# The last image's tail of a four-layer convolution kernel: sums by known means, a three-stage output loop, expert weights in halves

## The chip, the cores and the metric

The kernel runs on one core of a Trainium2 chip. Its time is the time on the device in microseconds (us), the median of several runs. All arithmetic is fp32. The engines are TensorE (PE in the profile; its weight loads are PEld), VectorE (DVE), ScalarE (ACT), GpSimd (POOL) and SyncE (SP), which issues most of the transfers.

## The reference

The input is x of shape (4, 256, 64, 64): four images of 256 channels and 4096 pixels. Four layers follow each other, each of the form `x = x + layer(gn(x))`, where `gn` normalises groups of 8 channels.

```python
def _gn(v, G=32, eps=1e-5):
    g = v.reshape(B_, G, C_ // G, H_, W_)
    return ((g - mean(g)) / sqrt(var(g) + eps)).reshape(v.shape)

# layer 0: 3x3 convolution, group norm of 8 groups, relu, then attention over the 4096 pixels
xs = relu(group_norm(conv3x3(x)));  attn = softmax(theta(xs)^T phi(xs));  y = attn g(xs)
layer0 = group_norm(conv1x1(y)) * 0.1 + xs
# layer 1: rmsnorm, qkv, linear attention of 4 heads, output product, rmsnorm
q = softmax(q, over head dim);  k = softmax(k, over pixels)
layer1 = rmsnorm(w_out @ (context(k, v) applied to q * scale))
# layer 2: per-image depthwise 3x3 taps and a 1x1 product, both generated from pooled hidden values
layer2 = einsum('bchw,boc->bohw', depthwise3x3(x, dk), pk) + bias
# layer 3: a mixture of 4 experts, mixed per image from the pooled input
alpha = softmax(relu(mean(x) @ w1.T) @ w2.T)
layer3 = einsum('boc,bchw->bohw', sum_k alpha_k experts_k, x)
```

## The kernel before, in words

Channels lie on the 128 partitions in two halves (`h`, NH = 2), and an image of 4096 pixels along the free dimension. PSUM is one pool of eight banks of 128x512 (`bank`). SBUF work tiles come from pools: `k4` (128x1024, nine buffers), `k2` (128x512, five). The order of the work is written out by hand, under a manual schedule: each layer is a Python generator that emits instructions and yields a number, and the class `Chain` turns the yielded numbers into steps of credit. `run` advances one chain by a step whenever the attention of another image advances by one. So attention of image b (1024 pf and 1024 py matmuls over the four images) is interleaved with the tail of image b-1 (layers 0's end to 3) and the convolution of image b+1. What a generator yields therefore decides beside which attention step its later work stands.

In `attend` (L885 to L948) a step is two pf matmuls (L895), two exponentials (L896), two py matmuls (L934) and a VectorE addition into tot (L124).

`Chain` also has a list of held products. The products of layer 3 of image 2, sixteen pieces of 128x512, are kept there; `fill(n)` emits the matmuls of n of them (L1357), and a later `settle()` their VectorE additions (res) and output transfers. They are emitted at fixed places of the last image's tail, which has no attention beside it.

The last image's tail keeps its convolution output in `x_cols`, inside the tile xp (argument `xs_in`), and its running image in tpg. It has these stages:

- `nonlocal_out` (L952 to L987): group statistics of the attention output (`group_finish`, L330: bn_aggr, matmul pm, matmul pv, a root on POOL, L217), then for each of eight parts of 1024 columns `stt` (wy times sc plus xs, a residual sum into big, here tpg) and two bn_stats (L984), whose statistics `linear_attention` needs.
- `linear_attention` (from L990): a loop of ps_qkv products, then the output loop. In it `outputs(c)` (L1086) makes four ps_o matmuls into two banks, four ScalarE squares with an accumulated sum (L1094), and the root of the sums (zr: VectorE L1096, POOL L217). `scaled` (L1100) multiplies by the root into z; in the last tail (`alone`) ScalarE does bank 0 and VectorE bank 1. `added` (L1110) transposes z (ps_zt, L1115), adds it to the image and takes bn_stats, for each half h. The order of a turn is outputs(c), added(c-1), scaled(c), settle, and after c = 2 and 4 a fill of one held product.
- `generated` (L1138): hidden products ps_h, normalised copies into xp, pooled values, taps dk; then for parts of the image the depthwise taps on VectorE (`taps`) or by diagonal matmuls (ps_dw), the weights pk from slices wp2 that SP loads, and the 1x1 products ps_pw.
- `mixed` (L1301): pooled values, alpha, expert weights wm by VectorE from the loaded experts ex, a bias b3 through the matmul ps_b (L1348), and sixteen output pieces: two ps_ex matmuls (L1357), the VectorE addition res, and an output transfer by SP.

For images 0 to 2 the same functions run beside attention, without `xs_in`, `diag` and `alone`; the expert mix of image 2 goes to `held`.

The statement that advances the output loop of a tail is this one:

```python
        last = None
        for c in range(NC):
            zb = outputs(c)
            yield 0.6
            if last is not None:
                added(c - 1, last)
            last = scaled(*zb)
            w.settle()
            if c in (2, 4):
                w.fill(1)
            yield 0.6
```

Of the kernel before, what the change touches and what calls it, by code (L numbers as in the profile page):

```python
# [8 lines left out]
F32 = mybir.dt.float32  # L9
AF = mybir.ActivationFunctionType  # L10
# [3 lines left out]
P = 128  # L14
# [79 lines left out]
def conv_preact_fast(ctx: ExitStack, tc: tile.TileContext, guard, x, wc, wtpg, ww, wqkv, wout, w1cat, wd2,  # L94
# [235 lines left out]
    def group_finish(st, avg, eps, shift=None):  # L330


        mv = sp.tile([P, NH, 2], F32, name="mv")
        for h in range(NH):
            nc.vector.bn_aggr(mv[:, h, :], st[:, h, :, :].rearrange("p c s -> p (c s)"))
        if shift is not None:
            tt(mv[:, :, 0], mv[:, :, 0], shift, ALU.add)
        yield 1
        pm = bank("pm")
        nc.tensor.matmul(pm[:, 0:NH], avg, mv[:, :, 0], start=True, stop=True)  # L340
        gm = sp.tile([P, NH], F32, name="gm")
# [608 lines left out]


    def nonlocal_out(w, b, big, k4, xs_in):  # L952
# [19 lines left out]
        _, gm, rstd = yield from group_finish(wy_stats[b], avg32, 1e-5, bias)  # L972
        sc, sh = affine(gm, rstd, vec_s[:, V_G2W, :], vec_s[:, V_G2B, :], bias, 0.1)
        st = stats_tile()
        w.fill(2)
        for i, (c, h) in enumerate(PARTS):
            cols = bass.ts(c, CH)
            wy, xs = parts[i]
            stt(big[:, h, cols], wy, sc[:, h:h + 1], xs, ALU.mult, ALU.add)
            if i + ahead < len(PARTS):  # L980
                parts.append(load_parts(i + ahead))
            yield 0.6
            for s in range(2):
                nc.vector.bn_stats(st[:, h, 2 * c + s, :], big[:, h, bass.ts(2 * c + s, 512)])  # L984
            yield 0.6
# [4 lines left out]
    def linear_attention(w, b, big, qT, k4, st, sh, alone):  # L990
# [95 lines left out]
        def outputs(c):  # L1086
            zr = sp.tile([P, 4], F32, name="zr", bufs=3)
            banks = []
            for s in range(2):
# [5 lines left out]
                banks.append(ps)  # L1095
            nc.vector.tensor_scalar(zr, zr, 1e-24, None, ALU.max)  # L1096
            rsqrt(zr, zr)
            return zr, banks

        def scaled(zr, banks):  # L1100
            z = k4("z").rearrange("p (j o) -> p j o", j=4)
            for s in range(2):
                if alone and s == 0:
                    for j in range(2):
                        nc.scalar.activation(z[:, j, :], banks[0][:, j, :], AF.Copy, scale=zr[:, j:j + 1])
                    continue
# [3 lines left out]
        def added(c, z):  # L1110
            cols = bass.ts(c, 512)
            for h in range(NH):
# [5 lines left out]

        last = None
        for c in range(NC):  # L1120
            zb = outputs(c)
            yield 0.6
# [9 lines left out]
        w.fill(2)  # L1132
# [5 lines left out]
    def generated(w, b, big, k4, st, sh, diag):  # L1138
# [126 lines left out]
        w.settle()  # L1265
# [4 lines left out]
        for n, i in enumerate(mine):  # L1270
# [9 lines left out]
            if n == 0:  # L1280
                for j in range(R):
# [19 lines left out]
    def mixed(w, b, big, k4, st, sh, held):  # L1301
# [29 lines left out]
        wm = k2("wm")  # L1331
        for j in range(NE):
            if j == 0:
                nc.vector.tensor_scalar(wm, ex[j // 2][:, j % 2, :], al[:, 0:1], None, ALU.mult)
            else:
                stt(wm, ex[j // 2][:, j % 2, :], al[:, j:j + 1], wm, ALU.mult, ALU.add)
            yield 0.5

        mix = wm.rearrange("p (h o) -> p h o", h=NH)
# [5 lines left out]
        pb3 = bank("ps_b3")  # L1345
        for oh in range(NH):
            for h in range(NH):
                nc.tensor.matmul(pb3[:, oh:oh + 1], wm[h][:, bass.ts(oh, P)], off[:, h:h + 1],  # L1348
                                 start=(h == 0), stop=(h == NH - 1))
        b3 = sp.tile([P, NH], F32, name="b3")  # L1350
        tt(b3, sh, pb3[:, 0:NH], ALU.subtract)

        def product(c, oh):
            cols = bass.ts(c, 512)
            ps = bank("ps_ex")
            for h in range(NH):
                nc.tensor.matmul(ps, wm[h][:, bass.ts(oh, P)], big[:, h, cols], start=(h == 0), stop=(h == NH - 1))  # L1357

            def added():
                res = k2("res")  # L1360
# [3 lines left out]

        w.settle()
        for c in range(N // 512):
            for oh in range(NH):
                if held is not None:
                    held.append(lambda c=c, oh=oh: lambda added=product(c, oh): added()())
                else:  # L1370
                    w.later(1, product(c, oh)())
                    yield 0.1
# [39 lines left out]
    with tc.manual_schedule(engines={E.PE, E.Activation, E.DVE, E.Pool, E.SP}):  # L1412
# [19 lines left out]
        last = end.steps()  # L1432
        while next(attention, False):
            pass
# [592 lines left out]
```

## Time and profile before

| | |
|---|---|
| median of 3 runs | 3117.1 us |
| the runs | 3116.27, 3117.1, 3123.15 us |
| the profiled execution | 3122.35 us |
| its span, first to last instruction | 3120.6 us |
| mean granted clock of TensorE | 0.987 |
| busy: PE, DVE, ACT, POOL | 3005.0, 2129.1, 1138.5, 131.1 us |
| instructions: PE, DVE, ACT, POOL | 8606, 2700, 2100, 178 |

The busy time of an engine is the sum of its instructions' durations. Since instructions overlap a little on VectorE and ScalarE, the pace of a row of equal instructions is shorter than one duration, and both are used here. A matmul of 128x512 in fp32 shows as two records. In the timeline, a line gives the start, the duration (of all that are merged), the engine, the source line, the operation, output and inputs, and in square brackets how long the engine was idle before it and what ended that. The clock is a share of full speed.

### The profile page before, as it was taken

The page shows a single profiled execution, that of the slowest core. Times are in us where ns is not written, and L with a number is a line of the kernel's source. Part 1 is how long each engine was busy: PE and PEld are TensorE (multiplying, and loading weights), DVE is VectorE, ACT ScalarE, POOL GpSimd, SP SyncE. Part 2 cuts the span into 40 slices and gives each one's busy share as a digit, 9 for nine tenths or more (in the row PEclk, how much of TensorE's full clock was granted, in tenths as well). Part 3 has the DMA queues.
Part 4 walks back from the last instruction along what each step waited for, and adds up shares of the span by engine and source line. Part 5 has one row for each costly group of instructions (what it writes and reads, how often), then busy time and mean ns, then how long its engine had stood idle before and what let it go on. Part 6 is the DMA issues. An engine that isn't in the chain of part 4 may idle for free.

```text
span 3120.6 us, 24280 instructions
## 1 busy us (share of the span) xinstructions
PE 3005.0 (96%) x8606; PEld 1487.8 (48%) x8606; DVE 2129.1 (68%) x2700; ACT 1138.5 (36%) x2100; POOL 131.1 (4%) x178
## 2 busy tenths in 40 slices
PE   6899999999999999999999999999999999996888
PEld 3354555445554444444565444444555544443533
DVE  8747777853557986786537896878353768855485
ACT  2134333353545332223454432322355453333510
POOL 0100000000110000000001000000000100000100
PEclk9999999999999999999999999999999999998999
DMA  5233111032001023113200102310510010120011
GB/s 217 80 101 136 37 48 35 26 59 88 33 11 34 7 74 125 41 44 81 88 11 1 41 29 86 104 41 24 128 48 1 11 41 7 47 74 34 14 61 65
DMA packets 58912, 174.25 MB, mean 56 GB/s; under 512 B 6432, under 2 KB 16416, under 8 KB 54560
## 3 DMA queue, kind: packets, MB, share of 16 engines
q1 hardware_dynamic: 54752, 155.85, 14.5%
q0 software_dynamic: 4032, 16.78, 2.9%
q8 instruction: 70, 1.15, 0.1%
q14 instruction: 58, 0.48, 0.0%
HBM read 111.26 MB, written 78.12 MB: 61 GB/s over the span
## 4 chain that ended last, share of the span: by engine, by line
PE 76%; DVE 17%; issue 5%; ACT 1%; POOL 0%; DMA 0%; POOLq 0%; ACTq 0%; DVEq 0%
PE pf L895 22%; PE py L934 22%; PE ps_qkv L1024 5%; PE ps_conv L496 4%; DVE dw L127 4%; PE ps_tp L871 4%; PE ps_ex L1357 3%; DVE tot L124 3%; PE ps_pw L1219 3%; PE ps_conv L568 2%; PE ps_g L876 2%; PE ps_wy L918 1%; PE ps_o L1092 1%; DVE big L127 1%; PE ps_ctx L1046 1%
## 5 line engine op out<-in xcount | busy, mean ns | idle before, releaser
L896 ACT ACTIVATE pr<-pf 128x512 f32<-128x512 f32 x1024 | 603.7, 597 | 1194.1 <-PE pf L895 1148.6
L895 PE MATMUL pf<-tpg 128*128 128x512 f32 x2048 | 968.8, 595 | 1.5 <-ACT pr L896 1.5
L934 PE MATMUL py<-pr,tpg 128*128 128x512 f32 x2048 | 962.1, 592 | 3.0 <-ACT pr L896 2.9
L124 DVE TENSOR_TENSOR tot<-tot,pr 128x1024 f32<-128x1024 f32 x448 | 546.4, 1220 | 182.6 <-ACT pr L896 181.3
L934 PEld LDWEIGHTS py<-pr,tpg 128*128 128x128 f32 x2048 | 388.9, 190 | 494.7 <-issue 478.3
L895 PEld LDWEIGHTS pf<-tpg 128*128 128x128 f32 x2048 | 382.0, 190 | 436.1 <-issue 411.4
L127 DVE SCALAR_TENSOR_TENSOR dw<-xp,dk,dw 128x1008 f32<-128x1008 f32 x216 | 273.0, 1268 | 6.8 <-ACT dw L1211 3.7
L496 PE MATMUL ps_conv<-v,u 128*128 128x512 f32 x384 | 170.8, 592 | 0.0
L1024 PE MATMUL ps_qkv<-wqkv_s,xg 128*128 128x384 f32 x384 | 129.9, 487 | 0.0
L124 DVE TENSOR_TENSOR tpg<-ps_g,bg_s 128x512 f32<-128x512 f32 x32 | 22.1, 692 | 145.6 <-PE ps_g L876 145.6
L871 PE MATMUL ps_tp<-big,wtpg_s 128*128 128x512 f32 x256 | 118.1, 605 | 3.0 <-ACT big L668 3.0
L496 PEld LDWEIGHTS ps_conv<-v,u 128*128 128x128 f32 x384 | 72.8, 190 | 92.2 <-issue 91.2
L217 POOL TENSOR_TENSOR rstd<-rstd,half 128x2 f32<-128x2 f32 x24 | 16.8, 700 | 2375.5 <-DVE rstd L351 2181.1
L1219 PE MATMUL ps_pw<-dw,pk 128*128 128x512 f32 x224 | 104.6, 601 | 8.1 <-DVE dw L127 8.1
L909 DVE RECIPROCAL inv<-pss 128x512 f32<-128x512 f32 x32 | 107.3, 3352 | 7.1 <-PE pss L907 7.1
L1024 PEld LDWEIGHTS ps_qkv<-wqkv_s,xg 128*128 128x128 f32 x384 | 72.2, 190 | 53.6 <-issue 9.3
L1034 DVE TENSOR_REDUCE qs<-qk 128x16 f32<-128x512 f32 x24 | 16.5, 686 | 118.6 <-ACT qk L1028 118.6
L872 ACT ACTIVATE tpg<-ps_tp,btp_s 128x512 f32<-128x512 f32 x64 | 43.8, 687 | 119.6 <-PE ps_tp L871 119.6
L871 PEld LDWEIGHTS ps_tp<-big,wtpg_s 128*128 128x128 f32 x256 | 47.9, 195 | 55.0 <-issue 50.6
L1094 ACT ACTIVATE junk<-ps_o 128x256 f32<-128x256 f32 x128 | 49.2, 384 | 67.5 <-PE ps_o L1092 59.4
L1219 PEld LDWEIGHTS ps_pw<-dw,pk 128*128 128x128 f32 x224 | 43.0, 192 | 62.6 <-issue 52.0
L1028 ACT ACTIVATE qk<-ps_qkv,rinv 128x256 f32<-128x256 f32 x96 | 45.6, 475 | 72.4 <-PE ps_qkv L1024 61.6
(309 smaller groups left out, 3120.7 us busy)
## 6 DMA issues: line engine op xcount, KB each, us to landing
xp<-in_x_dram SPq DMA_DIRECT2D x16, 1024.0 KB, 6.3
wy_d<-wt SPq DMA_DIRECT2D x32, 512.0 KB, 3.0
out_dram<-res SPq DMA_DIRECT2D x64, 256.0 KB, 2.0
wy<-wy_d SPq DMA_DIRECT2D x28, 512.0 KB, 4.7
xs_d<-big POOLq DMA_DIRECT2D x24, 512.0 KB, 11.0
u<-filters SPq DMA_DIRECT2D x48, 256.0 KB, 2.5
xs<-xs_d SPq DMA_DIRECT2D x24, 512.0 KB, 5.3
u<-rows_d SPq DMA_DIRECT2D x36, 256.0 KB, 3.1
```

The source lines that it names most:

```text
L124: nc.vector.tensor_tensor(o, a, b, op)
L127: nc.vector.scalar_tensor_tensor(o, a, s, b, op0, op1)
L496: nc.tensor.matmul(ps[oh], u(oh, h), v[:, bass.ts(h, 512)], start=(h == 0), stop=(h == NH - 1))
L568: nc.tensor.matmul(ps[:, bass.ts(oh, IY * IX)], u[i][:, h, bass.ts(oh, P)], v[:, i, bass.ts(h, IY * IX)], start=(h == 0), stop=(h == NH - 1))
L871: nc.tensor.matmul(ps, wtpg_s[:, h, k, :], big[:, h, cols], start=(h == 0), stop=(h == NH - 1))
L895: nc.tensor.matmul(pf, phi[:, bass.ts(2 * m + s, P)], theta[:, bass.ts(q, 512)], start=True, stop=True)
L896: nc.scalar.activation(pr[:, bass.ts(s, 512)], pf, AF.Exp)
L909: nc.vector.reciprocal(inv, pss)
L934: nc.tensor.matmul(py, g[:, bass.ts(2 * m + s, P)], probs[i][:, bass.ts(s, 512)], start=(m == 0 and s == 0), stop=(m == NM - 1 and s == 1))
L1024: nc.tensor.matmul(ps[:, 0:3 * HID], xg[:, h, bass.ts(j, P)], wqkv_s[:, h, :], start=(h == 0), stop=(h == NH - 1))
L1219: nc.tensor.matmul(ps, pk[:, h * NH * P + oh * P:h * NH * P + (oh + 1) * P], dw[h][:, bass.ts(s, 512)], start=(h == 0), stop=(h == NH - 1))
L1357: nc.tensor.matmul(ps, wm[h][:, bass.ts(oh, P)], big[:, h, cols], start=(h == 0), stop=(h == NH - 1))
```

## The change

It has five parts.

1. In the last attention, a generator `residual_sums` has ScalarE copy each 512 columns of `x_cols` to a scratch tile with an accumulated sum, three times in each attention step; VectorE adds the sixteen sums into res_sum.
2. In `nonlocal_out` of the last image, the mean of the residual sum is formed from known means before the sum itself. After each of the eight sums ScalarE takes the squares about that mean with an accumulator. The sixteen bn_stats and the bn_aggr are gone; `group_finish` calls `moments` in their place.
3. The output loop of the last image has three stages: outputs(c+1), scaled(c), added(c-1). The root of c+1 stands between the two halves of added(c-1). ScalarE scales three quarters (j = 0, 1, 2), VectorE one.
4. In `generated` the held results are settled after the first part's taps and no longer ahead of them.
5. In `mixed`, for all images, alpha times rstd is formed first, and the weights in two halves of four operations on 256 columns. For images without `held`, the first four banks get the products of half 0, then the bias product, then half 1.

```diff
     def group_finish(st, avg, eps, shift=None):
-        mv = sp.tile([P, NH, 2], F32, name="mv")
-        for h in range(NH):
-            nc.vector.bn_aggr(mv[:, h, :], st[:, h, :, :].rearrange("p c s -> p (c s)"))
+        if callable(st):
+            mv = st()
+        else:
+            mv = sp.tile([P, NH, 2], F32, name="mv")
+            for h in range(NH):
+                nc.vector.bn_aggr(mv[:, h, :], st[:, h, :, :].rearrange("p c s -> p (c s)"))
...
+    def residual_sums(xs_in):
+        parts = sp.tile([P, NH, N // 512], F32, name="res_parts", bufs=1)
+        for h in range(NH):
+            for c in range(N // 512):
+                nc.scalar.activation(junk(), xs_in[:, h, bass.ts(c, 512)], AF.Copy, accum_out=parts[:, h, c:c + 1])
+                yield
+        nc.vector.tensor_reduce(res_sum, parts, AX.X, ALU.add)
...
+        if xs_in is not None:
+            tt(mv[:, :, 0], wmv[:, :, 0], bias, ALU.subtract)
+            tt(mv[:, :, 0], mv[:, :, 0], sc, ALU.mult)
+            stt(mv[:, :, 0], res_sum, 1.0 / N, mv[:, :, 0], ALU.mult, ALU.add)
+            nc.vector.tensor_scalar(centre, mv[:, :, 0], -1.0, None, ALU.mult)
+
+            def moments():
+                nc.vector.tensor_reduce(mv[:, :, 1], squares, AX.X, ALU.add)
+                nc.vector.tensor_scalar(mv[:, :, 1], mv[:, :, 1], 1.0 / N, None, ALU.mult)
+                return mv
+            st = moments
...
-            for s in range(2):
-                nc.vector.bn_stats(st[:, h, 2 * c + s, :], big[:, h, bass.ts(2 * c + s, 512)])
+            if xs_in is not None:
+                nc.scalar.activation(wy, big[:, h, cols], AF.Square, bias=centre[:, h:h + 1], accum_out=squares[:, h, c:c + 1])
+            else:
+                for s in range(2):
+                    nc.vector.bn_stats(st[:, h, 2 * c + s, :], big[:, h, bass.ts(2 * c + s, 512)])
...
+            if alone:
+                for j in range(4):
+                    src = banks[j // 2][:, j % 2, :]
+                    if j < 3:
+                        nc.scalar.activation(z[:, j, :], src, AF.Copy, scale=zr[:, j:j + 1])
+                    else:
+                        nc.vector.tensor_scalar(z[:, j, :], src, zr[:, j:j + 1], None, ALU.mult)
+                return z
...
+        if alone:
+            this, last = outputs(0), None
+            root(this[0])
+            for c in range(NC):
+                after = outputs(c + 1) if c + 1 < NC else None
+                z = scaled(*this)
+                for h in range(NH):
+                    if last is not None:
+                        added(c - 1, last, (h,))
+                    if h == 0 and after is not None:
+                        root(after[0])
+                this, last = after, z
+                w.settle()
+                if c in (2, 4):
+                    w.fill(1)
+                yield 1
+            added(NC - 1, last)
+            w.fill(2)
+            return st
...
         dw = {mine[0]: centre(mine[0])}
-        w.settle()
...
             if n == 0:
+                w.settle()
                 for j in range(R):
...
-        wm = k2("wm")
-        for j in range(NE):
-            if j == 0:
-                nc.vector.tensor_scalar(wm, ex[j // 2][:, j % 2, :], al[:, 0:1], None, ALU.mult)
-            else:
-                stt(wm, ex[j // 2][:, j % 2, :], al[:, j:j + 1], wm, ALU.mult, ALU.add)
-            yield 0.5
...
-            nc.vector.tensor_scalar(wm[h], mix[:, h, :], rstd[:, h:h + 1], None, ALU.mult)
-        yield 1
+        for h in range(NH):
+            nc.vector.tensor_scalar(scales[:, h, :], al, rstd[:, h:h + 1], None, ALU.mult)
...
+            for j in range(NE):
+                e = ex[j // 2].rearrange("p k (h o) -> p k h o", h=NH)[:, j % 2, h, :]
+                if j == 0:
+                    nc.vector.tensor_scalar(wm[h], e, scales[:, h, 0:1], None, ALU.mult)
+                else:
+                    stt(wm[h], e, scales[:, h, j:j + 1], wm[h], ALU.mult, ALU.add)
+                if j % 2 == 1:
+                    yield 0.6
+        yield 0.5
...
+        first = [bank("ps_ex") for _ in range(4)]
+        for h in range(NH):
+            for ps, (c, oh) in zip(first, pieces):
+                multiply(ps, c, oh, h)
+            if h == 0:
+                bias()
+        for ps, (c, oh) in zip(first, pieces):
+            w.later(1, adder(ps, c, oh)())
+            yield 0.1
...
+        sums = residual_sums(x_cols)
         while next(attention, False):
+            for _ in range(3):
+                next(sums, None)
+        for _ in sums:
             pass
```

More of the change, by code (lines that the diff above doesn't have):

```diff
@@ L948, in attend @@
                 yield
+    res_sum = cp.tile([P, NH], F32, name="res_sum")
+    def residual_sums(xs_in):
[5 more added lines that the diff above has]
+        nc.vector.tensor_reduce(res_sum, parts, AX.X, ALU.add)
     def nonlocal_out(w, b, big, k4, xs_in):
@@ L971, in nonlocal_out @@
         bias = vec_s[:, V_WB, :]
-        _, gm, rstd = yield from group_finish(wy_stats[b], avg32, 1e-5, bias)
+        wmv, gm, rstd = yield from group_finish(wy_stats[b], avg32, 1e-5, bias)
         sc, sh = affine(gm, rstd, vec_s[:, V_G2W, :], vec_s[:, V_G2B, :], bias, 0.1)
         st = stats_tile()
+        if xs_in is not None:
+            mv = sp.tile([P, NH, 2], F32, name="mv_in", bufs=1)
+            centre = sp.tile([P, NH], F32, name="centre", bufs=1)
+            squares = sp.tile([P, NH, N // CH], F32, name="squares", bufs=1)
+            tt(mv[:, :, 0], wmv[:, :, 0], bias, ALU.subtract)
[7 more added lines that the diff above has]
+            st = moments
         w.fill(2)
@@ L1095, in outputs, with root, added @@
                 banks.append(ps)
+            return zr, banks
+        def root(zr):
             nc.vector.tensor_scalar(zr, zr, 1e-24, None, ALU.max)
             rsqrt(zr, zr)
-            return zr, banks
         def scaled(zr, banks):
             z = k4("z").rearrange("p (j o) -> p j o", j=4)
+            if alone:
[6 more added lines that the diff above has]
+                return z
             for s in range(2):
[L1103 to L1106, printed above, removed]
                 tt(z[:, bass.ts(s, 2), :], banks[s], zr[:, bass.ts(s, 2)].unsqueeze(2).to_broadcast([P, 2, NH * P]), ALU.mult)
             return z
-        def added(c, z):
+        def added(c, z, halves=range(NH)):
             cols = bass.ts(c, 512)
-            for h in range(NH):
+            for h in halves:
                 pt = bank("ps_zt")
@@ L1121, in linear_attention @@
             zb = outputs(c)
+            root(zb[0])
             yield 0.6
@@ L1131, in linear_attention @@
         added(NC - 1, last)
-        w.fill(2)
         return st
@@ L1330, in mixed @@
         w.fill(3)
-        wm = k2("wm")
-        for j in range(NE):
-            if j == 0:
-                nc.vector.tensor_scalar(wm, ex[j // 2][:, j % 2, :], al[:, 0:1], None, ALU.mult)
-            else:
-                stt(wm, ex[j // 2][:, j % 2, :], al[:, j:j + 1], wm, ALU.mult, ALU.add)
-            yield 0.5
-        mix = wm.rearrange("p (h o) -> p h o", h=NH)
+        scales = sp.tile([P, NH, NE], F32, name="scales")
+        for h in range(NH):
+            nc.vector.tensor_scalar(scales[:, h, :], al, rstd[:, h:h + 1], None, ALU.mult)
+        mix = k2("wm").rearrange("p (h o) -> p h o", h=NH)
         wm = []
@@ L1342, in mixed, with bias, multiply, adder @@
             wm.append(mix[:, h, :] if held is None else filter_tile("wmh")[:, 0, :])
-            nc.vector.tensor_scalar(wm[h], mix[:, h, :], rstd[:, h:h + 1], None, ALU.mult)
-        yield 1
[L1345 to L1349, printed above, removed]
-        b3 = sp.tile([P, NH], F32, name="b3")
[L1351 to L1357, printed above, removed]
+            for j in range(NE):
[7 more added lines that the diff above has]
+        yield 0.5
+        b3 = sp.tile([P, NH], F32, name="b3")
+        def bias():
+            pb3 = bank("ps_b3")
+            for oh in range(NH):
+                for h in range(NH):
+                    nc.tensor.matmul(pb3[:, oh:oh + 1], wm[h][:, bass.ts(oh, P)], off[:, h:h + 1],
+                                     start=(h == 0), stop=(h == NH - 1))
+            tt(b3, sh, pb3[:, 0:NH], ALU.subtract)
+        def multiply(ps, c, oh, h):
+            nc.tensor.matmul(ps, wm[h][:, bass.ts(oh, P)], big[:, h, bass.ts(c, 512)], start=(h == 0), stop=(h == NH - 1))
+        def adder(ps, c, oh):
             def added():
-                res = k2("res")
+                res, cols = k2("res"), bass.ts(c, 512)
                 stt(res, ps, b3[:, oh:oh + 1], big[:, oh, cols], ALU.add, ALU.add)
@@ L1363, in product @@
             return added
-        w.settle()
[L1366 to L1372, printed above, removed]
+        def product(c, oh):
+            ps = bank("ps_ex")
+            for h in range(NH):
+                multiply(ps, c, oh, h)
+            return adder(ps, c, oh)
+        pieces = [(c, oh) for c in range(N // 512) for oh in range(NH)]
+        if held is not None:
+            bias()
+            for c, oh in pieces:
+                held.append(lambda c=c, oh=oh: lambda added=product(c, oh): added()())
+            return
+        w.settle()
+        first = [bank("ps_ex") for _ in range(4)]
+        for h in range(NH):
+            for ps, (c, oh) in zip(first, pieces):
+                multiply(ps, c, oh, h)
+            if h == 0:
+                bias()
+        for ps, (c, oh) in zip(first, pieces):
+            w.later(1, adder(ps, c, oh)())
+            yield 0.1
+        for c, oh in pieces[4:]:
+            w.later(1, product(c, oh)())
+            yield 0.1
     def tail(b, big, qT, k4=k4, diag=None, xs_in=None, held=None):
```

## The prediction

> **What bounds the kernel now.** First I read the page's slices.
>
> ```profile
> PE   6899999999999999999999999999999999996888
> DVE  8747777853557986786537896878353768855485
> ```
>
> TensorE (PE) is full from slice 3 to 36, 78 us each, while attention of one image runs beside other work of its neighbours: there only a stall of TensorE costs time. Only the end, the last image's tail, has room. So I took the busy time by stage, cut at the tail's own borders.
>
> ```profile
> 2600.00:2800.00 200.00, 200.00 (x479) 89.18 (x478) 149.00 (x159) 69.17 (x118) 0.70 (x1) 1.00 0.13 44
> ...
> 2829.00:2851.30 22.30, 1.77 (x6) 0.46 (x4) 21.91 (x31) 0.00 (x0) 0.00 (x0) 0.64 0.13 49
> 2851.30:2922.60 71.30, 66.49 (x299) 45.97 (x299) 21.11 (x51) 46.95 (x97) 9.20 (x17) 0.92 0.01 5
> 2922.60:2970.00 47.40, 37.33 (x144) 24.77 (x145) 30.36 (x55) 21.37 (x80) 8.06 (x8) 0.86 0.07 23
> 2970.00:3013.60 43.60, 33.00 (x114) 14.32 (x112) 37.48 (x53) 12.57 (x23) 0.74 (x2) 0.95 0.30 108
> 3013.60:3073.00 59.40, 57.13 (x126) 24.83 (x126) 51.98 (x60) 3.39 (x5) 0.00 (x0) 0.95 0.00 0
> ```
>
> Columns: start:end, length, busy PE, weight loads, DVE (VectorE), ACT (ScalarE), POOL, then TensorE's clock. The residual sum (2829 to 2851.3) is VectorE alone, ScalarE at zero: room for the first part of the change. In the output loop (2922.6 to 2970) nobody is full, so a cycle of waits sets it, which the timeline shows:
>
> ```profile
> 2929.93 0.17 DVE L1096 TENSOR_SCALAR zr<-zr 128x4 f32<-128x4 f32 x1 [2.07 <-ACT junk L1094]
> ...
> 2930.18 1.01 POOL L217 TENSOR_TENSOR zr<-zr,half 128x4 f32<-128x4 f32 x1 [3.04 <-DVE zr L1096]
> ...
> 2931.23 0.84 ACT L1105 ACTIVATE z<-ps_o,zr 128x256 f32<-128x256 f32 x2 [1.33 <-POOL zr L217]
> ...
> 2933.99 0.17 DVE L1096 TENSOR_SCALAR zr<-zr 128x4 f32<-128x4 f32 x1 [0.53 <-ACT junk L1094]
> ...
> 2934.22 3.49 PE L1357 MATMUL ps_ex<-big,wmh 128*128 128x512 f32 x4
> ```
>
> zr to zr is 4.06 us: root on VectorE and POOL 1.30, two ScalarE scales 0.73, four squares 2.06. The two turns with a held product are 6.7 us: the product stands ahead of the next ps_o and runs at half clock, 3.49 for what takes 1.72 elsewhere.
>
> **What the Trainium skill says.** "PSUM — Partial Sum Buffer", section "PSUM bank collisions raise a hardware error": two engines must be kept apart on one bank, two readers too. Before, ScalarE reads one bank of ps_o and VectorE the other, and both start at 2927.18; no run yet shows them on one bank. "TensorE: Matmul & The Clock Gate", Part 1: an idle window of about 3.4 us halves the clock. The trace agrees: matmuls stop at 2830.8 and the clock of 2835 to 2838 averages 0.56. In the loop it falls to 0.56 at 2934 to 2937, after 3.4 us with only transposes.
>
> **The change part by part.**
>
> *Input sums.* 16 ScalarE activations of 128x512 with an accumulator join the last attention, three a step. Priced by L913 (0.63, the accumulator's 0.19 read starting at +0.54): 0.73 each, 2.2 for three. Two exponentials take 1.2; a step is 3.43. They fit by a hair, and TensorE asks for the exponentials a step later: cost 0, bound 0 to +0.5. Without that cover they would cost 11.7.
>
> *Mean and centre.* Four dependent tiny VectorE operations ahead of the first residual sum, 0.20 apart as L342 to L351 show, the last overlapped: **+0.65**.
>
> *Residual sum.* Before, 2829.07 to the pm matmul at 2851.28 is 22.2: eight sums at 1.30, sixteen bn_stats at 0.60, two held results 1.3, aggregation 0.8. After, ScalarE squares each 1024 columns: 1.056 (L1002) plus 0.09 for a per-partition operand (L1211's 1.148) plus 0.13 for the accumulator (pace 0.515 against 0.384 on 256 columns), 1.28. The first starts at +1.33, the eighth ends at +11.5; VectorE's own eight sums and two results end at +11.0 to +11.8; reduce, scale and shift 0.6. 12.4: **-9.8** (-10.6 to -8.6, the square's price being unmeasured). VectorE's row is bounded below by 9.6, so ScalarE's pace is late next. The loads of parts 6 and 7 land about 2832, needed at 2837.
>
> *Output loop.* The program as built has VectorE's quarter wait for ScalarE's third: the quarters j=2 and j=3 lie in one bank. On VectorE stand quarter(c), added(c-1, half 0), root(c+1), added(c-1, half 1). So root(c+1) comes after scaled(c), and the cycle is root and POOL 1.30, three scales 1.21 (0.37+0.37+0.47), hand-over 0.05, quarter 0.26, stt 0.77, bn_stats 0.61: **4.20 us, no shorter than 4.06**. What goes is the held products' 2.7 twice: TensorE's 1.72 of ps_o and 0.86 of transposes leave 1.6 a turn. Summed from w at 2922.63: zr(0) +3.25 as before; then four squares of outputs(1) 2.06, scales 1.21 and the quarter 0.3 bring zr(1) to +6.8; POOL 1.3 (squares(2) end at the same time as it does or later, +8.5), scales 1.2, quarter 0.3, one half of added(0) 1.4 bring zr(2) to +11.4; five turns of 4.2 to +32.4; held results +0.4, last scaling 2.8, four halves at 1.38, aggregation 0.8: pm at +42.0 against 47.4, **-5.4**. The last two held products start cold at about +36, 5.3 long as before, and just fit. If the clock still falls, -1; without the bank wait, -12.
>
> *Held results moved (generated).* Four results of 0.67 leave the place ahead of the first taps. Taps start when centre ends, 2982.95, not at 2986.60; the results then follow, at 2993.4 to 2996.1, so pk starts at 2996.1 instead of 2996.94: -0.8. But on SP the wp2 loads 2 and 3 now stand behind four output DMAs that wait for those results. Before, all four were issued by 2989. Load 2 is now issued about 2996.3 and lands 3.3 or more later (this load: 3.3/4.5/7.1); pk's fifth operation, due 2999.2, waits some 1.3. Net **+0.5** (-0.8 to +2.5).
>
> *Expert weights in halves.* Eight operations of 256 columns for four of 512 and two of 256. In the last tail, TensorE still has three held products to 3084.9, while weights end at 3082.5 now: the cover is there on both sides, and the four ps_b matmuls (0.8) stay in its queue. **0** (-0.8 to +0.4).
>
> *The same edit in images 1 and 2.* Its yields move later work on the attention steps: in the built order the first ps_conv of the next image comes one step (a pf and a py group, 3.43) earlier.
>
> ```profile
> 1250.97 1.23 DVE L127 SCALAR_TENSOR_TENSOR ra<-xp,ra 128x1024 f32<-128x1024 f32 x1
> 1251.57 1.88 PE L895 MATMUL pf<-tpg 128*128 128x512 f32 x4
> 1252.12 1.22 DVE L124 TENSOR_TENSOR tot<-tot,pr 128x1024 f32<-128x1024 f32 x1
> ...
> 1253.25 2.35 DVE L124 TENSOR_TENSOR v<-ra 128x1024 f32<-128x1024 f32 x2
> 1253.29 1.88 PE L934 MATMUL py<-pr,tpg 128*128 128x512 f32 x4
> ...
> 1255.00 7.03 PE L496 MATMUL ps_conv<-v,u 128*128 128x512 f32 x16
> ```
>
> TensorE would reach ps_conv at 1251.57, but ra ends 1252.2 and v, put ahead of tot, 1253.4: it stands 1.9. All that follows is late by it. The ps_b wait of 0.35 goes: +1.6. A regrouped pf may wait for its bank (0 to 0.9): +2.0 each, **+4.0** (+2 to +8).
>
> *Sum.* +0.65 -9.8 -5.4 +0.5 +4.0 = **-10.0** on the profiled execution's 3122.35 (span 3120.6). That lies 5.3 above the median, within the runs' spread of 3116.27 to 3123.15, so I take the difference off the median: 3117.1 - 10.0 = **3107.1 us**. This measurement tells about 0.2%, 6.2 us, from no change.
>
> **The rivals.**
>
> *Loop truly overlapped* (1 in 10). If both engines read the bank freely, ScalarE's 2.06+1.1 and VectorE's 3.1 set 3.2 a turn; seven turns save 7 more: 3100. The ScalarE rows speak for it, the built wait against.
>
> *Gains eaten before the tail* (17 in 100). Stalls in images 1 and 2 at their +8 and the loop cold (-1) give -10.0+4+4.4, about -2: 3115, no change. For it: TensorE full there and VectorE 157 of 200 us busy; against: later ps_conv groups stand as before.
>
> *Phase shift that lasts* (11 in 100), the slower side. If in both images each of the 24 ps_conv passes, not only the first, now waits for VectorE, then 48 waits of x count in full: zero gain at x = 0.21, at 0.35 +6.8: 3124. For it: before, v ends only about 0.5 ahead of its ps_conv. Against: the built order is the same again after two groups.
>
> *It does not do what it says*: that is my forecast for the loop, whose three stages keep the two-stage cycle.
>
> **How the numbers follow.** The forecast has 62 in 100, alone 3103 to 3111; most of it, and the first rival, is beyond 6.2 us: faster 0.68. The second rival and the forecast's weak end: same 0.20; the third: slower 0.12. The range runs from the overlapped loop's side, 3099, to 3117, leaving out the third rival.
>
> **What would show it.** In the changed profile: bn_stats L984's successor gone between residual sums, ScalarE squares about 1.28 apart, pm some 13 us after the first affine; zr to zr 4.2 with VectorE's quarter waiting for ScalarE, TensorE's clock 1.0 in the loop until the last held products; a wait of VectorE at pk for a DMA; TensorE waiting about 2 us for v at the first ps_conv of images 1 and 2. zr spacing near 3.2, or waits at later ps_conv, would prove me wrong.

## The result, and the profile after

| | before | after |
|---|---|---|
| median of 20 runs each, us | 3119.2 (3116.3 to 3124.2) | 3114.2 (3112.4 to 3115.5) |
| profiled execution, us | 3122.35 (span 3120.6) | 3113.03 (span 3111.2) |
| ratio after to before, 95% interval | | 0.998 (0.9974 to 0.9986) |

The change makes the kernel faster by 5.0 us, 0.16%. The interval lies wholly below 1, so the gain is not scatter, but it is smaller than the 0.2% that the prediction set as its bound. The two profiled executions differ by 9.3 us, where the sum of steps said 10.0. Where the difference between 9.3 and 5.0 lies is the main question of what follows.

The page's slices of the kernel after, TensorE's row:

```profile
PE   6899999999999999999999999999999999998888
```

Little is to be seen at 78 us a slice: one PE slice of the end is 8 instead of 6. The stretches are what tells. This is the busy time by stretch (columns: start:end, length, busy PE, weight loads, VectorE, ScalarE, POOL, TensorE's clock, DMA share, GB/s). First the kernel before, then the kernel after, cut at the same events: the residual sum, ps_qkv to w, the output loop, ps_h to the pooling matmul, and the first ps_pw that waits for VectorE to the last pm.

```profile
2829.07:2851.28 22.21, 1.68 (x5) 0.39 (x3) 21.84 (x30) 0.00 (x0) 0.00 (x0) 0.64 0.12 48
2855.42:2922.63 67.21, 65.34 (x295) 45.00 (x295) 20.10 (x44) 46.09 (x96) 8.44 (x15) 0.95 0.00 1
2922.63:2970.04 47.41, 37.37 (x144) 24.77 (x145) 30.33 (x55) 21.37 (x80) 8.06 (x8) 0.86 0.07 23
2973.25:2980.36 7.11, 7.11 (x49) 2.62 (x46) 6.19 (x11) 4.23 (x8) 0.00 (x0) 1.00 0.19 74
3013.60:3073.10 59.50, 57.13 (x127) 24.86 (x127) 51.98 (x60) 3.39 (x5) 0.00 (x0) 0.95 0.00 0
```

```profile
2833.53:2844.97 11.44, 3.98 (x6) 1.35 (x5) 11.35 (x14) 9.61 (x16) 0.00 (x0) 0.65 0.17 66
2849.17:2916.78 67.61, 65.74 (x295) 45.14 (x295) 20.08 (x44) 46.03 (x96) 8.43 (x15) 0.94 0.00 1
2916.78:2959.76 42.98, 35.00 (x144) 22.58 (x145) 28.74 (x55) 24.10 (x88) 8.05 (x8) 0.92 0.07 25
2963.00:2971.81 8.81, 8.81 (x49) 3.08 (x47) 6.19 (x11) 4.23 (x8) 0.00 (x0) 0.81 0.53 180
3007.14:3063.62 56.48, 54.20 (x123) 23.83 (x123) 51.57 (x60) 3.39 (x5) 0.00 (x0) 0.97 0.00 0
```

Laid beside the profile of before, event by event:

| stretch | before | after | difference |
|---|---|---|---|
| start to last ps_wy (images 0 to 2, attention) | 2821.5 | 2825.2 | +3.6 |
| ps_wy to the first residual sum | 7.55 | 8.38 | +0.8 |
| residual sum, to its pm | 22.21 | 11.44 | -10.8 |
| pm to ps_qkv | 4.14 | 4.20 | +0.1 |
| ps_qkv to w | 67.21 | 67.61 | +0.4 |
| output loop, w to pm | 47.41 | 42.98 | -4.4 |
| pm to ps_h, and ps_h to the pooling matmul | 3.21 + 7.11 | 3.24 + 8.81 | +1.7 |
| pooling matmul to the first ps_pw that waits for VectorE | 33.2 | 35.3 | +2.1 |
| from there to the last pm | 59.50 | 56.48 | -3.0 |
| last pm to the end | 47.50 | 47.58 | +0.1 |

In the residual sum VectorE (11.35 of 11.44 us) and ScalarE (9.61) now stand side by side. The timeline shows the pace:

```profile
2834.73 1.28 DVE L127 SCALAR_TENSOR_TENSOR tpg<-wy,sc,xp 128x1024 f32<-128x1024 f32 x1
2834.85 1.15 ACT L1014 ACTIVATE ra<-tpg,centre 128x1024 f32<-128x1024 f32 x1 [7.09 <-DVE tpg L127]
...
2835.93 1.28 DVE L127 SCALAR_TENSOR_TENSOR tpg<-ra,sc,xp 128x1024 f32<-128x1024 f32 x1
2836.04 1.15 ACT L1014 ACTIVATE wy<-tpg,centre 128x1024 f32<-128x1024 f32 x1
```

VectorE's sums come every 1.19 us, and each square starts as its sum ends. ScalarE keeps that pace, so a square of 1024 columns with its accumulator's read costs at most 1.19 here.

One turn of the output loop after:

```profile
2928.07 0.15 DVE L1132 TENSOR_SCALAR zr<-zr 128x4 f32<-128x4 f32 x1
2929.40 1.20 ACT L1141 ACTIVATE ra<-ps_o,zr 128x256 f32<-128x256 f32 x3 [1.34 <-POOL zr L217]
2930.71 0.48 DVE L1143 TENSOR_SCALAR ra<-ps_o,zr 128x256 f32<-128x256 f32 x1 [1.11 <-ACT ra L1141]
2931.11 0.74 DVE L127 SCALAR_TENSOR_TENSOR tpg<-ps_zt,gains,tpg 128x512 f32<-128x512 f32 x1
...
2932.50 0.15 DVE L1132 TENSOR_SCALAR zr<-zr 128x4 f32<-128x4 f32 x1
```

Root, three scales on ScalarE, VectorE's quarter (which waits 1.11 for them), half of added, root: 4.43 us here, 4.43 to 4.46 in all turns but the first, none of them longer for a held product. In the kernel before, five of the seven turns took 4.05 to 4.12 and the two with a held product 6.7 to 6.8. So the ordinary turn has become longer, and the gain of the loop is mainly the two long turns that are gone.

Next, TensorE's stall at a first ps_conv (one of two such stalls), and VectorE's at pk:

```profile
1250.62 1.23 DVE L124 TENSOR_TENSOR v<-ra 128x1024 f32<-128x1024 f32 x1
...
1251.90 3.70 PE L499 MATMUL ps_conv<-v,u 128*128 128x512 f32 x8 [1.78 <-DVE v L124]
```

```profile
2985.55 2.31 SPq L1425 DMA_DIRECT2D out_dram<-res  x4
...
2987.41 3.11 DVE L127 SCALAR_TENSOR_TENSOR pk<-wp,pb,pk 128x512 f32<-128x512 f32 x4
...
2987.95 0.91 SPq L1220 DMA_DIRECT2D wp<-in_wp_dram  x2
...
2993.64 3.11 DVE L127 SCALAR_TENSOR_TENSOR pk<-wp,pb,pk 128x512 f32<-128x512 f32 x4 [3.12 <-DMA wp<-in_wp_dram]
```

SP issues four output transfers, then the two wp2 loads; the first lands 5.7 us after its issue, and VectorE stands 3.12 us.

### The profile page after: what moved, and what is told of

Read it like the earlier page. It is cut to its first block, busy times and chain, and to the rows that moved or that the text cites. A ratio compares the mean times of both kernels' runs of the same rounds, so it can differ in the third digit from the quotient of the medians.

```text
span 3111.2 us, 24363 instructions
## 1 busy us (share of the span) xinstructions
PE 3007.1 (97%) x8606; PEld 1486.8 (48%) x8606; DVE 2119.0 (68%) x2705; ACT 1160.4 (37%) x2156; POOL 131.0 (4%) x178
## 4 chain that ended last, share of the span: by engine, by line
PE 77%; DVE 16%; issue 5%; ACT 1%; DMA 0%; POOL 0%; POOLq 0%; SPq 0%; DVEq 0%; ACTq 0%
PE pf L898 22%; PE py L937 22%; PE ps_qkv L1057 5%; PE ps_conv L499 4%; DVE dw L127 4%; PE ps_tp L874 4%; PE ps_ex L1419 3%; DVE tot L124 3%; PE ps_pw L1279 3%; PE ps_conv L571 2%; PE ps_g L879 2%; PE ps_wy L921 2%; PE ps_o L1125 1%; DVE ra L127 1%; DVE big L127 1%
## 5 line engine op out<-in xcount | busy, mean ns | idle before, releaser
L874 PEld LDWEIGHTS ps_tp<-big,wtpg_s 128*128 128x128 f32 x256 | 47.5, 193 | 54.3 <-issue 49.8
L1127 ACT ACTIVATE junk<-ps_o 128x256 f32<-128x256 f32 x128 | 49.1, 384 | 63.7 <-PE ps_o L1125 59.4
```

What stands on the lines that cost most here:

```text
L874: nc.tensor.matmul(ps, wtpg_s[:, h, k, :], big[:, h, cols], start=(h == 0), stop=(h == NH - 1))
```

## The experiments

Ratios are against runs of the kernel before on the same chip in the same session. The kernel after was timed once, beside the result, so a difference from its 3114.2 is one between sessions.

### The kernel before, unchanged

The times of the kernel before lie in two bunches; without that the median can't be understood. In the 20 runs beside the result they are plain: eleven lie from 3116.3 to 3120.1 (median 3117.0) and nine from 3122.4 to 3124.2 (median 3123.2). Of all 96 runs on record, 51 lie up to 3121.2 and 45 from 3121.7 on, and there the gap is only 0.5 wide. No edit:

> The kernel before, unchanged, once more. Its times fall into two groups, near 3117 and near 3123, and the profile that the prediction was built on belongs to the upper one. Clock theory: the groups differ in the last image's output loop, where TensorE's clock falls in some executions and not in others. If this profile is of the lower group, w to the pm after the loop takes 42 to 44 us at a clock above 0.93 instead of 47.4 at 0.86, and all other stages are within 0.5 of the first profile; if it is of the upper group, 47.4 again. Rival: the loop takes 47.4 in both groups and the 6 us lie in another stage.

> The kernel before, unchanged, looked at a third time. The two profiles so far are of the upper group of its times (3122.4 and 3124.0) and agree within 0.1 us in every stage of the last tail. Clock theory: a profile of the lower group has the first products of linear attention (ps_qkv to w) at 65.4 instead of 67.2 and one turn with a held product at 5.1 instead of 6.8, as the kernel with the residual sum alone showed; together 3.5 of the 5 to 6 us between the groups. Rival: those stages stay at 67.2 and 47.4 and the difference lies elsewhere.

Their profiled executions took 3124.0 and 3122.5 us, that of the prediction 3122.35: all belong to the upper bunch. So the first run's theory was not tested: the profile that would have shown a shorter loop did not come. In every stretch from the residual sum to the last pm the three agree within 0.1 us; from the last pm to the end they take 47.5, 48.5 and 48.1. Of before_again, ps_qkv to w (67.21 in the first):

```profile
2856.03:2923.31 67.28, 65.41 (x295) 45.01 (x295) 20.11 (x44) 46.09 (x96) 8.45 (x15) 0.95 0.00 1
```

No profile shows the lower bunch, but the mean granted clock of each execution is on record for 76 of the 96 runs, and it parts the bunches. All 40 runs up to 3121.2 have 0.988 or 0.989, all 36 above it 0.986 or 0.987. The means of the two groups differ by 0.0014 in the clock and by 4.2 us in the time; 0.0014 of 3120 us is 4.3 us (an estimate). So the bunches go with the clock, and the size fits. In which stretch the clock differs, this doesn't show; before_warm, below, tries it in another way.

### One part alone

The input sums, the mean and centre, and the centred squares put into the kernel before, all else as it was:

```diff
+            if xs_in is not None:
+                nc.scalar.activation(wy, big[:, h, cols], AF.Square, bias=centre[:, h:h + 1], accum_out=squares[:, h, c:c + 1])
+            else:
+                for s in range(2):
+                    nc.vector.bn_stats(st[:, h, 2 * c + s, :], big[:, h, bass.ts(2 * c + s, 512)])
...
+            for _ in range(3):
+                next(sums, None)
```

> The kernel before with the input sums and the centred squares alone (old loop, old expert weights). Steps-add theory: from the last ps_wy to the first ps_qkv 24.0 us instead of 33.9, nothing given back, so 9.9 off each group of the kernel before: near 3107 and 3113, median about 3110. Rival (what was gained here is eaten later, by the loads of the tail or by the loop): 3114 or more, with a later stage longer than before by over 2 us.

Measured: 3108.2 (3107.8 to 3108.7), ratio 0.9959 (0.9945 to 0.9972): five runs within 0.9 where two groups were expected, 11.8 below the kernel before, and 6 below the whole change. From ps_wy to ps_qkv it takes 23.8, so the steps-add theory holds for the stretch. Two later stretches, whose instructions are those of before, are shorter too (the rows of before are 67.21 and 47.41):

```profile
2845.18:2910.61 65.43, 63.55 (x295) 43.90 (x295) 20.10 (x44) 45.82 (x96) 8.43 (x15) 0.97 0.00 1
2910.61:2956.26 45.65, 35.63 (x144) 24.25 (x145) 30.35 (x55) 21.34 (x80) 8.05 (x8) 0.89 0.07 24
```

The clock column rises with it. From the first ps_qkv on the clock is at half for 3.66 us here and for 7.28 in the kernel before; in each pair of rows below, the first is the cold part. One of the two turns with a held product takes 5.1 instead of 6.8. So of the 13.6 between this profile and that of before, 3.5 is these two stretches, which the full change doesn't have.

```profile
2845.18:2848.84 3.66, 3.66 (x10) 2.31 (x10) 0.69 (x1) 3.60 (x5) 0.00 (x0) 0.50 0.00 0
2848.84:2852.50 3.66, 3.66 (x15) 2.34 (x16) 0.76 (x2) 1.74 (x5) 1.01 (x1) 1.00 0.00 0
```

```profile
2855.42:2862.70 7.28, 7.28 (x17) 4.72 (x18) 1.46 (x3) 4.96 (x8) 1.01 (x1) 0.50 0.00 0
2862.70:2866.36 3.66, 3.66 (x18) 2.47 (x18) 0.53 (x1) 2.46 (x7) 0.00 (x0) 1.00 0.00 0
```

The output loop alone in the kernel before:

```diff
+        if alone:
+            this, last = outputs(0), None
+            root(this[0])
+            for c in range(NC):
+                after = outputs(c + 1) if c + 1 < NC else None
+                z = scaled(*this)
...
```

> The kernel before with the three-stage output loop alone (results still settled ahead of the taps, old expert weights). Clock theory: w to pm 43.0, zr to zr 4.46, one group of times in place of two, at 3115 to 3117: 4.4 to 7 below the upper group, 0 to 2 below the lower. Rival (the loop's gain is real in every execution): 4.4 or more below both groups, 3112.5 to 3118.5 in two groups, median 4.4 or more below the kernel before on the same chip.

Measured: 3116.9 (3114.1 to 3119.0), ratio 0.9986 (0.9977 to 0.9994), -3.1. The loop took 42.97 as in the full change. The expected single bunch did not come: the runs spread over 4.9 us, so the loop is not the only seat of the two bunches. Two stretches moved that hold no line of the loop, ps_h to the pooling matmul (7.11 before) and from the first waiting ps_pw to pm (59.50 before):

```profile
2968.99:2977.80 8.81, 8.81 (x49) 3.11 (x47) 6.19 (x11) 4.34 (x8) 0.00 (x0) 0.81 0.16 60
3011.04:3067.20 56.16, 53.88 (x123) 23.75 (x123) 51.48 (x60) 3.39 (x5) 0.00 (x0) 0.97 0.00 0
```

So the +1.7 and -3.0 of the full change belong to the loop. The +1.7 is a fall of the clock at ps_h. In the kernel after:

```profile
2956.50:2963.00 6.50, 3.44 (x20) 1.52 (x22) 4.33 (x16) 0.00 (x0) 0.74 (x2) 1.00 0.00 0
2963.00:2966.50 3.50, 3.50 (x27) 1.20 (x28) 3.25 (x6) 0.00 (x0) 0.00 (x0) 0.51 0.05 17
```

It is not the dip of the last turns (0.56 from 2948.5 to 2956.0, where TensorE has mostly transposes), which is over before pm; it comes after the 3.2 us in which TensorE has little but pm, pv and ps_b. The kernel before has the same wait there and stays at 1.00, so why the loop brings the dip is open. Of the -3.0, 1.7 is work that has moved: 48 records of ps_dw run ahead of the first ps_pw, where before there were 44, at 0.42 us each. Probably this is because the loop yields other numbers; that was not tried alone. The other 1.3 is fewer matmuls at half clock after the wait (0.97 against 0.95 in the clock column).

### The digit that places ps_conv

```diff
                 if j % 2 == 1:
                     yield 0.6
-        yield 0.5
+        yield 0.6
```

> The changed kernel with one digit changed: the expert weights' last yield is 0.6 in place of 0.5, which puts the first ps_conv of images 1 and 2 back on the attention step where it stood before. Stall theory: TensorE's two waits of 1.8 us for v go, the last ps_wy comes at 2821.5 to 2822.3 in place of 2825.2, and the time is 3.0 to 3.7 lower than the changed kernel's 3114.2, about 3110.7. Rival (the weights' other placing, eight short operations, is what costs): ps_wy stays at 2824 or later and the time at 3113 to 3114.

Measured: 3107.0 (3106.6 to 3108.3), ratio 0.9955 (0.9942 to 0.9969). The time falls by 7.2, twice what was expected. TensorE's waits in the attention, of the full change and of this kernel (us in total, times, longest):

```profile
PE ps_conv L499 <- DVE v L124: 3.6, 2, 1.8
PE pf L898 <- ACT pr L899: 2.9, 4, 0.7
```

```profile
PE pf L898 <- ACT pr L899: 1.5, 2, 0.7
```

ps_conv's waits are gone and two of pf's four. In the profiles the last ps_wy comes at 2819.7 instead of 2825.2, -5.4: 3.6 for ps_conv, 1.4 for pf, against 0.6 more for py; the other 1.0 is not resolved (ps_wy of the unchanged kernel comes at 2821.2 to 2821.7). The other 1.8 of the median's 7.2 is no stretch at all: the full change's profiled execution lies 1.2 below its median, that of yield06 0.6 above.

### The wp2 loads and the results

```diff
             if n == 0:
-                w.settle()
                 for j in range(R):
...
                         slices.append(load_wp2(j // 2 + 2))
+                    if j == R // 2 - 1:
+                        w.settle()
                     yield 0.35
```

> The changed kernel with the held results of the generated stage settled after pk's fourth operation, where wp2 loads 2 and 3 have been issued, and no longer ahead of pk; so on SP these loads stand ahead of the four output transfers. Queue theory: pk's wait of 3.1 us for its fifth operation goes; the first ps_pw that waits for VectorE comes 3.1 earlier, TensorE is full from there, so the time is 3.1 lower than the changed kernel's 3114.2: 3111.1. Rival (TensorE had ps_dw matmuls to do in the wait, so the wait is free): 3114 with a longer idle stretch ahead of that ps_pw.

Measured: 3110.7 (3109.6 to 3111.5), 3.5 below the full change. pk no longer waits, the results fill the place:

```profile
2985.75 3.11 DVE L127 SCALAR_TENSOR_TENSOR pk<-wp,pb,pk 128x512 f32<-128x512 f32 x4
2988.78 2.72 DVE L127 SCALAR_TENSOR_TENSOR res<-ps_ex,b,big 128x512 f32<-128x512 f32 x4
2991.42 3.11 DVE L127 SCALAR_TENSOR_TENSOR pk<-wp,pb,pk 128x512 f32<-128x512 f32 x4
```

From w to the waiting ps_pw it takes 87.2 instead of 90.4, as the queue theory said; the stretch after it is unchanged (56.6).

### What sets the loop's cycle

Root moved ahead of VectorE's quarter, and, in another kernel, the quarters dealt so that VectorE shares no bank with ScalarE's first two scales:

```diff
+                if after is not None:
+                    root(after[0])
                 z = scaled(*this)
-                for h in range(NH):
-                    if last is not None:
-                        added(c - 1, last, (h,))
-                    if h == 0 and after is not None:
-                        root(after[0])
+                if last is not None:
+                    added(c - 1, last)
```

```diff
-                for j in range(4):
+                for j in (0, 2, 3, 1):
                     src = banks[j // 2][:, j % 2, :]
-                    if j < 3:
+                    if j > 0:
```

> The changed kernel with root(c+1) issued ahead of scaled(c) in the output loop, so that VectorE clamps zr before it takes its quarter and both halves of added(c-1). Queue theory (the cycle of 4.46 comes from where root stands on VectorE): zr to zr 3.4 to 3.5, set by ScalarE's four squares and three scales (3.3) and VectorE's 3.4; six turns save 6 us: w to pm 37, time near 3108. Rival (the shared bank sets the cycle, root's place is of no account): 4.3 or more a turn, time 3113 to 3114. Rival 2 (another queue, TensorE's or the PSUM banks, is late next): between, 3.7 to 4.1.

> The changed kernel with the quarters dealt otherwise: VectorE takes j=0 and does it first, ScalarE takes 2, 3 (the other bank) and then 1, so that VectorE no longer waits for ScalarE's third scale; root stays where it was. Bank theory (the wait of VectorE's quarter for its bank sets the cycle): zr to zr 3.3 to 3.5 and w to pm 36 to 37, time near 3108. Rival (the quarter's wait is not on the cycle): 4.2 to 4.5 a turn, 3114.

root_ahead: 3111.5 (3109.5 to 3112.3), loop 39.3; after a first turn of 2.0, zr to zr alternates between 3.0 to 3.7 and 4.3 to 5.0, a mean of 4.0, so the middle rival fits; which queue is late was not followed up. VectorE's quarter still waits up to 1.00 for ScalarE's third scale, and now has both halves of added behind that wait.

quarter_first: 3106.1 (3104.0 to 3106.6), loop 35.1, zr to zr 3.1 to 3.2 in the turns without a held product's work in the way, 3.9 to 4.1 in the others:

```profile
2923.58 0.48 DVE L1143 TENSOR_SCALAR z<-ps_o,zr 128x256 f32<-128x256 f32 x1 [1.12 <-POOL zr L217]
...
2925.13 1.20 ACT L1141 ACTIVATE z<-ps_o,zr 128x256 f32<-128x256 f32 x3
2925.38 0.15 DVE L1132 TENSOR_SCALAR zr<-zr 128x4 f32<-128x4 f32 x1
```

The quarter now starts on POOL's word, and the next root is clamped while ScalarE still scales. That one reordering takes 7.9 from the loop, so the cycle ran through the wait for the shared bank. Root's place counts too: with the wait still there, root_ahead took 3.7.

### The clock held up by idle-time matmuls

TensorE is given matmuls that nothing reads, in the kernel before:

```diff
             stt(big[:, h, cols], wy, sc[:, h:h + 1], xs, ALU.mult, ALU.add)
+            if warm is not None and i >= 0:
+                for _ in range(3):
+                    nc.tensor.matmul(warm, ident, big[:, h, bass.ts(2 * c, 512)], start=True, stop=True)
...
+        if alone:
+            warm = bank("ps_warm")
+            for _ in range(4):
+                nc.tensor.matmul(warm, ident, big[:, 0, 0:512], start=True, stop=True)
...
                 pt = bank("ps_zt")
+                if alone and c < NC:
+                    nc.tensor.matmul(pt, ident, qT[:, 0:512], start=True, stop=True)
```

> The kernel before with idle-time matmuls added that nothing reads: three of 128x512 after each residual sum, four after the pv matmul ahead of linear attention, one ahead of the transposes of each half in the output loop. They keep TensorE busy where it stood idle. Clock theory of the two groups of times: with the clock at 1.0 from the first ps_qkv on, ps_qkv to w takes 63.7 instead of 67.2, the two long turns of 6.7 to 6.8 shrink to 4.1 to 5.2, the profiled time falls by 6 to 7 to about 3116, and the times lie within 2 us of each other instead of in two groups 5 to 6 apart. Rival (the groups come from elsewhere in the kernel): all times fall alike and still lie in two groups.

Measured: 3119.7 (3117.7 to 3120.9, 13 runs), ratio 0.9998 (0.9989 to 1.0006); about 3116 was expected. Residual sum, ps_qkv to w and output loop:

```profile
2828.16:2851.97 23.81, 23.81 (x55) 10.36 (x54) 21.84 (x30) 0.00 (x0) 0.00 (x0) 0.96 0.15 59
2856.91:2920.57 63.66, 61.78 (x296) 42.76 (x294) 20.11 (x44) 44.45 (x95) 8.45 (x15) 1.00 0.00 1
2920.57:2965.47 44.90, 42.57 (x176) 27.56 (x177) 30.50 (x54) 21.66 (x80) 8.06 (x8) 1.00 0.07 24
```

With the clock at 1.00, ps_qkv to w takes 63.66 (63.7 expected). The turns with a held product take 6.0, so of their extra 2.7 only a part was clock; here the added matmuls fill TensorE too. The gain is paid back: the added matmuls end 1.6 and 0.8 too late for pm and ps_qkv, ps_h is cold afterwards (8.8), and the end takes 1.7 more than in the prediction's profile (0.7 more than in before_again). But the two bunches are gone: 13 runs lie within 3.2 us, where the same number of runs of before_again spread over 6.2, and all have a clock of 0.993 or 0.994. Together with the clocks on record this supports the clock as the cause of the bunches; that the added matmuls stilled something else as well is not excluded, and which dips the lower bunch lacks was not seen.

### The edits together

yield06, pk_loads and quarter_first in one kernel; then with idle-time matmuls, and with about half as many of them in three of the four places (this last run was on another chip, beside its own runs of the kernel before):

> The changed kernel with three edits of the earlier experiments together: the expert weights' last yield of 0.6, the held results settled after the wp2 loads, and VectorE's quarter first. Separate-places theory: the three gains are taken in three different stretches of one chain and add: 7.2 + 3.5 + 8.1 = 18.8 below the changed kernel's 3114.2, so 3095.4, with 3094 to 3097 as scatter. Rival (a stretch gives back what another gains, TensorE's clock first): 3098 or more, with ps_qkv to w or the stretch after ps_h longer by over 2 us than in the single experiments.

> The kernel of the run named best with idle-time matmuls that nothing reads: two after each of the last five residual sums, four after the pv matmul ahead of linear attention, one ahead of each half's transposes in the last three turns of the output loop, three ahead of ps_b and ps_h. Clock theory: ps_qkv to w 63.7 instead of 67.6, ps_h to the pooling matmul 7.1 instead of 8.8: 5.6 below best, about 3090. Rival (they stand in TensorE's queue ahead of pm, ps_qkv and the transposes and delay them by as much): within 1 us of best or slower.

> The kernel of the run named best_warm with about half of its idle-time matmuls: one after each of the last five residual sums, two (not four) after the pv matmul ahead of linear attention, two (not three) ahead of ps_b and ps_h; those in the output loop stay. In best_warm they ended 2.2 us too late for pm, 0.7 too late for ps_qkv and 1.2 too late for ps_b. Clock theory: half is still enough to hold the clock at 1.0, ps_qkv to w stays at 63.7, ps_h to the pooling matmul at 7.1, and these 4.1 us come free: 3091.4. Rival (too few to hold the clock): ps_qkv to w back at 67 to 68 and the time at 3095 or more.

| kernel | median (range), us | ratio to before (95%) |
|---|---|---|
| best | 3097.1 (3095.8 to 3098.3) | 0.9923 (0.9910 to 0.9937) |
| best_warm | 3095.5 (3094.9 to 3095.9) | 0.9919 (0.9906 to 0.9933) |
| best_warm_half | 3093.4 (3092.3 to 3094.0) | 0.9912 (0.9899 to 0.9926) |

best came 1.7 above the sum of the single gains: 17.1 of 18.8. In its profile the three stretches gain what they did singly (ps_wy -5.5, loop -7.8, pm to the waiting ps_pw -3.3: 16.6), and 0.7 is lost after them: the span is 15.9 shorter. So the separate-places theory holds by stretch. Its five times part by the clock as well: two at 3095.8 with 0.991, three from 3097.1 to 3098.3 with 0.989. In best_warm the clock stayed up but the matmuls stood in the way as the rival said (pm 2.2 late), and 1.6 of the expected 5.6 came; half as many held it nearly as well, and ended in time. The row of best_warm_half for ps_qkv to w (its residual sum takes 11.45, as without them):

```profile
2844.30:2908.47 64.17, 62.30 (x296) 43.02 (x294) 20.11 (x44) 44.98 (x95) 8.43 (x15) 0.99 0.00 1
```

It was expected at 3091.4. The 2 us that lack: 64.17 instead of 63.7, 57.6 instead of 56.6 from the waiting ps_pw to pm, and 0.7 of the delays ahead of ps_qkv and ps_b that stayed. At 3093.4 it is 26 us below the kernel before and 21 below the changed one.

## Why the prediction was right or wrong, point by point

**The sum against the profile: right, with luck in it.** -10.0 was forecast on 3122.35 and -9.3 came. Single terms were off by up to 1.6, two effects of -3.0 and +1.7 were not in it, and these errors cancelled.

**From the sum to the median: the step that failed.** "That lies 5.3 above the median, within the runs' spread, so I take the difference off the median." The profiled execution was of the upper bunch; 51 of 96 runs are of the lower. The kernel after has one bunch, and its median lies 1.2 above its profiled execution, where before's lies 3.2 below. 9.3 - 3.2 - 1.2 = 4.9 is what the medians show. A spread of 7 us in three runs was the sign that a single offset would not do: the sum belongs to the bunch of its profile. Left on the profile it gives 3112.35, 1.9 from the median that came, where 3107.1 is 7.1 off. Beside the result, the kernel after is 9.0 below the upper bunch's median and 2.8 below the lower one's. That the range still held the result is owed to its width, 10 us on the slow side, and not to this step; the chance of 68 in 100 for more than 6.2 us was too high by it.

In the points that follow, the first number is the forecast, the second what the stretch of the profile showed.

**Residual sum**, -9.8: -10.8. Term mis-sized: the pace was put at ScalarE's 1.28; VectorE's sums set it, at 1.19, and ScalarE was not late next. **Mean and centre**, +0.65: +0.6 (resid_alone) to +0.8. **Input sums**, 0: no later ps_wy in resid_alone, right.

**Output loop**, -5.4: -4.4, cycle 4.46 against 4.20. Terms: the quarter costs 0.40 to its successor, not 0.26, and the three scales to the quarter's start 1.31, not 1.26. The mechanism, a wait of two readers for one bank, was right and quarter_first shows it; the Trainium skill, "PSUM — Partial Sum Buffer", section "PSUM bank collisions raise a hardware error", asks for engines to be kept apart on a bank, and here the wait that keeps them apart cost 1.1 us a turn. That the three stages keep the two-stage cycle came as forecast. The clock was to stay at 1.0 until the last held products and did not: it was at 0.56 from 2948.5 on, ahead of them. Two effects of the loop were not in the sum at all: +1.7 at ps_h from a clock that falls anew there, and -3.0 after the wait at ps_pw, from ps_dw matmuls that moved ahead of it and fewer cold ones.

**Held results moved**, +0.5: +2.1. The wait for the wp2 load was named, with its place and its cause on SP, and sized at 1.3 from the load's fastest landing of 3.3; it landed after 5.7, behind four outputs, and the wait was 3.1. This is the largest term that was mis-sized.

**Expert weights**, 0 at the end: +0.1, less than the 1.0 by which this end varies between profiles of the kernel before. **In images 1 and 2**, +4.0: +3.6 at ps_wy, 1.78 a stall against 1.9. The ps_b wait that goes and pf's two new waits of 0.7 were both named. In the medians the placing costs more, 7.2 by yield06.

**By medians** the parts are: residual -11.8, loop -3.1, placing +7.2, results +3.5, together -4.2 against -5.0 measured. Most of what the residual sum gains was given back at two places that a digit and a line repair.

**The rivals.** The overlapped loop, turns of 3.2, came with quarter_first, and not with the change as it stands. Gains eaten before the tail (3115) is nearest in time, and its mechanism can't be put aside: in the profile the stalls were the forecast's +4, but undoing them gave 5.4 in the profile and 7.2 in the medians, close to its +8; and the loop did go cold at its end. The lasting phase shift did not come: only the first ps_conv of each image waits.

## What to carry to other kernels

Before a sum of steps is taken off a median, look at the single times: if they fall into bunches, say which one the profile belongs to. The granted clock of each execution can tell. When a step is moved, size its DMA by the landing behind what now stands ahead of it (5.7 us here), and not by the fastest seen (3.3). Where two engines share the reading of one PSUM bank, order the work so that the one with the longer queue behind it reads first: one reordering was worth more here (7.9) than the new loop (4.4).

## What the runs showed of the hardware

- How long TensorE stays at half clock after an idle stretch varies: from the first ps_qkv on it was 3.7 us (resid_alone), 7.3 (before), 8.1 (after) and 9.5 (loop_alone), and ps_qkv to w took 65.4, 67.2, 67.6 and 68.4, for the same instructions. The Trainium skill, "TensorE: Matmul & The Clock Gate", Part 1, says that the window runs freely and that the count of cold matmuls varies by its phase; the traces agree that it varies. It puts the sustained work that brings full clock at some 3.4 us, which only the shortest of the four is near; here the measurement decides. It puts the ramp at under 1% of a span, which holds here (0.1% at each place, an estimate from these times), but that is the size of what was to be measured.
- Executions of one unchanged kernel differ in their mean granted clock (0.986 to 0.989 in 76 runs), and their times part by it: up to 3121.2 us at 0.988 and above, from 3121.7 at 0.987 and below.
- Idle-time matmuls keep the clock up (1.00 and 0.99 from ps_qkv to w) and are worth 3.7 us net here if they end in time (best_warm_half against best, by medians from two chips). One of 128x512 after each of the last five residual sums, 1.19 us apart, with two more after pv, was enough for the 0.99.
